# Cross-attention on one core: the probabilities' transposition put ahead of the maxima, x in two buffers

## The chip, the cores and the metric

The kernel runs on one core of a Trainium2 chip. A core has a matrix engine (TensorE, "PE" in the profile; its weight loads are "PEld"), VectorE ("DVE"), ScalarE ("ACT"), GpSimd ("POOL") and SyncE ("SP"). Each of these works through its own list of instructions in order and waits on semaphores for the others. Data lies in SBUF (128 partitions), matrix products come out in PSUM, and DMA queues move data between SBUF and the chip's DRAM; in this kernel nearly all DMAs are issued by SP, whose list holds little else. The metric is the device time of one execution in microseconds (us).

## The reference

The reference is one cross-attention layer. x has 32 batches of 512 rows and 640 channels, the context 32 batches of 77 rows and 1024 channels, and there are 20 heads of 32 channels. With S = 512 and C = 640:

```python
def _sdpa(q, k, v):
    scale = 1.0 / np.sqrt(HD).astype(np.float32)
    s = jnp.einsum('bhqd,bhkd->bhqk', q, k) * scale
    p = jax.nn.softmax(s, axis=-1)
    return jnp.einsum('bhqk,bhkd->bhqd', p, v)
...
q = _heads(hidden_states @ to_q_w)
h_txt = _sdpa(q, _heads(ehs_txt @ to_k_w), _heads(ehs_txt @ to_v_w))
...
out = out @ to_out_w + to_out_b
out = (out + residual) / RESCALE
```

The three other branches (object, others, ip) take the context rows behind the first 77, and there are none, so they add nothing. All is fp32.

## The kernel before, in words

**Precision.** The large products (queries, keys, values of the context, output projection) split each operand into a rounded high part and the low rest, both of type fp32r, and add three products of the parts. ACT makes the high part (a cast), VectorE or POOL the low part (a subtraction).

**Stages.** First the keys and values of all 32 batches are computed and written to DRAM (`k_dram`, `v_dram`). Ahead of that stand matmuls on a tile of zeros (`warm`, L253), which wait for no data. Then comes the main part: a batch has 5 chunks of 128 channels (4 heads), and one chunk of one batch is a *slot*. Slots are numbered n = 0 to 159, with batch b = n div 5 and j = n mod 5; `slot(n)` writes the instructions of one slot, and every engine takes its share of them in the order written. A few instructions after the last slot (`end`) drain the pipeline.

**What a slot does, by the names that the profile uses:**

- `scores(n)` (L410): 32 small matmuls of queries `qt` and keys `kb` into four PSUM tiles `sc`, one for each head. There are only four such tiles, so the scores of a slot need the exponentials of the slot before to be through with them, and they need `copy_q`.
- `maxima(n)` (L422): four VectorE reductions into `nm`, the negated row maxima.
- `exps(n, i)` (L432): for each head 4 ACT exponentials with bias `nm`, each with an instruction that reads out the row sum; 16 of each a slot. Output goes to one of two tiles `pn`, by the parity of n.
- `sums(n)` (L442): a VectorE reciprocal of the row sums. `normalize(n)` (L447): one POOL multiplication over the whole of `pn`.
- `transpose_p(n)` (L454, L461): one VectorE transposition of `pn` in 32x32 blocks into the tile `z`, of which there is one, and four DMAs from `z` to a DRAM tile `pd`. `load_p(n)` (L470) reads `pd` back in one DMA as `raw`, keys on the partitions.
- `values(n)` (L478): 8 matmuls of `raw` and the values `vb` into `pa`; `high_a`, `low_a` (L492, L497) split the result.
- `queries(n + 1)` (L393): 15 matmuls of x and the query weights into `pq`, and `copy_q(n + 1)` (L402), which copies them to `qt` for the next slot: on ACT behind the exponentials in most slots, on VectorE in the first ones.
- `piece(...)` (L515): a part of the output projection of an earlier batch, two pieces a slot; `finish` (L544, L550) adds the residual with bias on VectorE and issues the store of the rows.
- x for the queries: `load_x` (L231) loads a batch in four quarters of 32 partitions, `transpose_x` (L235, VectorE) transposes it in place in four parts (slots j = 0 and 1), and `split_x` (ACT L242, POOL L243) makes the parts that the matmuls read (slots j = 2 and 3). One buffer holds x; a load of the next batch waits until the last split has read the one before.
- `load_residual`, `add_bias` (L504, L508): rows of x again, to which POOL adds the bias a slot later.

**Depth.** In slot n the scores are those of n, the queries those of n + 1, the transposition that of n - 1, `load_p` that of n - 2 and the values those of n - 3 (`taken`). Slots without a projection (`has_out` false: n = 0 to 6) are the *fill*; in slots 0 and 1 the rest of the context's values is computed as well.

**Order.** The scheduler is switched off for all engines (`tc.manual_schedule`), so the order in `slot` is the order on each engine, SP's queue included. In it the transposition of n - 1 stands behind the first half of the exponentials, on VectorE therefore directly behind the maxima of n.

Of the kernel before, what the change touches and what calls it, by code (L numbers as in the profile page):

```python
# [8 lines left out]
F32 = mybir.dt.float32  # L9
# [14 lines left out]
P = 128  # L24
Q = 32
# [12 lines left out]
def kernel(  # L38
# [26 lines left out]
    B, S, C = x.shape  # L65
# [3 lines left out]
    NC_ = C // P  # L69
# [148 lines left out]
    def context_values(g, j, pool):  # L218
        values_of(g, j, pool)
        split_values(g, j)  # L220

    xts, xss, xpool = {}, {}, []

    def load_x(b, quarters=range(4)):

        if b not in xss:
            xss[b] = xpool[0].tile([P, S // Q, C // 4], F32, tag="xs", name="xs")
        xs = xss[b]
        src = x[b].rearrange("(a j) (q u) -> q j a u", j=Q, q=4)
        for q in quarters:  # L230
            nc.sync.dma_start(xs[q * Q : (q + 1) * Q, :, :], src[q])  # L231

    def transpose_x(b, i):
        part = xss[b][:, 4 * i : 4 * i + 4, :].rearrange("p a u -> p (a u)")
        nc.vector.transpose(part, part)  # L235
# [13 lines left out]
    zero = kvt.tile([P, G], FPR, name="zero")  # L249
    nc.vector.memset(zero.bitcast(F32), 0.0)  # L250
    warm = psk.tile([P, G], F32, tag="ps", name="warm")
    for _ in range(12):
        nc.tensor.matmul(warm, zero[:, :P], zero, start=True, stop=True)  # L253

    def first(*ks):
# [126 lines left out]
    def load_keys(b):  # L382
        nc.sync.dma_start(kbs[b % 2], k_dram[:, :, b * NKEY : (b + 1) * NKEY])

    def load_values(b):
        nc.sync.dma_start(vbs[b % 2], v_dram[b * NKEY : b * NKEY + KPAD])

    def queries(n):
        b, j = divmod(n, NC_)
        pqs[n] = ps.tile([P, S], F32, tag="pq", name="pq", bufs=1)  # L390
        for k in range(NC_):
            for m, (a, c) in enumerate(PAIRS):
                nc.tensor.matmul(  # L393
                    pqs[n],
                    wq_s[:, k, a, j * P : (j + 1) * P],
                    xts[b, k][:, c, :],
                    start=(k == 0 and m == 0),
                    stop=(k == NC_ - 1 and m == 2),
                )

    def copy_q(n, copy=nc.scalar.copy):
        copy(qts[n % 2], pqs.pop(n))  # L402

    def scores(n):
        b, j = divmod(n, NC_)
        scs[n] = [ps.tile([P, NQ, P], F32, tag="sc", name="sc", bufs=4) for _ in range(HPC)]
        for t in range(NQ):
            for i, sc in enumerate(scs[n]):
                r = slice(i * HD, (i + 1) * HD)
                nc.tensor.matmul(  # L410
                    sc[:, t, :NKEY],
                    qts[n % 2][r, t * P : (t + 1) * P],
                    kbs[b % 2][r, j, :],
                    start=True,
                    stop=True,
                    tile_position=(i * HD, 0),
                )

    def maxima(n):
        nms[n] = main.tile([P, HPC, NQ], F32, tag="nm", name="nm", bufs=2)  # L420
        for i, sc in enumerate(scs[n]):
            nc.vector.tensor_reduce(  # L422
                nms[n][:, i], sc[:, :, :NKEY], AX.X, ALU.max, negate=True
            )

    def exps(n, i):
        if i == 0:
            sms[n] = main.tile([P, NQ * HPC], F32, tag="sm", name="sm", bufs=2)
        sc = scs[n][i]
        for t in range(NQ):  # L430
            at = t * HPC + i
            nc.scalar.activation(  # L432
                pnb[n % 2][:, at, :NKEY],
                sc[:, t, :NKEY],
                AF.Exp,
                bias=nms[n][:, i, t : t + 1],
                accum_out=sms[n][:, at : at + 1],
            )

    def sums(n):  # L440
        rss[n] = main.tile([P, NQ * HPC], F32, tag="rs", name="rs", bufs=2)
        nc.vector.reciprocal(rss[n], sms.pop(n))  # L442
# [8 lines left out]
    def transpose_p(n):  # L451

        pn = pnb[n % 2]
        nc.vector.transpose(  # L454
            z.rearrange("p b t j -> p t b j"),
            pn.rearrange("p (t h) k -> p t (h k)", t=NQ).rearrange("p t (b i) -> p t b i", i=Q),
        )
        pd = dram.tile([NBLK * Q, S], F32, tag="pd", name="pd", bufs=6)
        rows = pd.rearrange("(b i) q -> i b q", i=Q)
        for a in range(4):  # L460
            nc.sync.dma_start(  # L461
                rows[:, :, a * P : (a + 1) * P],
                z[a * Q : (a + 1) * Q].rearrange("p b t j -> p b (t j)"),
            )
        pds[n] = pd

    def load_p(n):
        pd = pds.pop(n)
        raw = late[0].tile([KPAD, HPC, S], F32, tag="raw", name="raw", bufs=2)
        nc.sync.dma_start(raw, pd.rearrange("(h k) q -> k h q", h=HPC))  # L470
        raws[n] = raw

    def values(n):
        b, j = divmod(n, NC_)
        raw, vb = raws.pop(n), vbs[b % 2][:, j]
        pas[n] = late[1].tile([P, S], F32, tag="pa", name="pa", bufs=1)
        for i in range(HPC):
            nc.tensor.matmul(  # L478
                pas[n][i * HD : (i + 1) * HD, :],
                vb[:, i, :],  # L480
                raw[:, i, :],
                start=True,
                stop=True,
                tile_position=(0, i * HD),
            )
# [15 lines left out]
    def load_residual(b, t, xr=None):  # L501
        if xr is None:
            xr = late[0].tile([P, C], F32, tag="xr", name="xr", bufs=4)
        nc.sync.dma_start(xr, x[b, t * P : (t + 1) * P, :])  # L504
        xrs[b, t] = xr

    def add_bias(b, t):
        nc.gpsimd.tensor_tensor(xrs[b, t], xrs[b, t], bias, ALU.add)  # L508
# [21 lines left out]
    def piece(b, i):  # L530
        for t, h, j in STEPS[CUTS[i] : CUTS[i + 1]]:
            if j == 0:
                output_bank(b, t, h)
            project(b, t, h, j)
            if j == NC_ - 1:
                closed.append((b, t, h))
# [36 lines left out]
    def slot(n, beside=()):  # L573
        b, j = divmod(n, NC_)
        ahead, more = n + 1 < N, b + 1 < B
        back, first = PIECES[j]
        bo_, has_out = b - back, b >= back
        xsplits = SPLIT_X.get(j, ()) if more and n > LATE else ()
        turns = TRANSPOSE_X.get(j, ((), ())) if more and b else ((), ())
        if b == 1 and j < 2:  # L580
            turns = (((), ()), ((0, 1), (2, 3)))[j]
        taken = takes.get(n)
        filling = not has_out

        scores(n)
        if taken is not None:
            values(taken)
        maxima(n)
        if n - LAG + 1 in pds and n > LATE:
            load_p(n - LAG + 1)  # L590
        for k in WO.get(n, ()):
            nc.sync.dma_start(wos[0][:, k].bitcast(F32), wo_dram[:, k].bitcast(F32))
        if j == 0 and more:
            load_keys(b + 1)
        if j == 1:
            load_values(b)
        if n == NC_:
            load_x(b + 1, (2, 3))
        if j == 4 and b and b + 2 < B:
            load_x(b + 2, (0, 1))  # L600
        if j in RESIDUAL and b >= RESIDUAL[j][0]:
            load_residual(b - RESIDUAL[j][0], RESIDUAL[j][1])
        if j in BIAS and b >= BIAS[j][0]:
            add_bias(b - BIAS[j][0], BIAS[j][1])
        if has_out:
            piece(bo_, first)
        for i in range(2):
            exps(n, i)
        if n:
            transpose_p(n - 1)  # L610
        finish()
        if j == 4 and b + 2 < B:
            load_x(b + 2, (0, 1) if not b else (2, 3))
        for i in turns[0]:
            transpose_x(b + 1, i)
        if len(beside) > 1:
            context_values(LAST, beside[1], psv)
        if ahead:
            queries(n + 1)
        if len(beside) > 0:  # L620
            context_values(LAST, beside[0], psv)
        if filling and ahead:
            copy_q(n + 1, nc.vector.tensor_copy)
        for i in range(2, HPC):
            exps(n, i)
        sums(n)
        normalize(n)
        if taken is not None:
            high_a(taken)
        if has_out and ahead:  # L630
            copy_q(n + 1)
        if has_out:
            piece(bo_, first + 1)
        if taken is not None:
            low_a(taken)
        for c in xsplits:
            split_x(b + 1, c)
        for i in turns[1]:
            transpose_x(b + 1, i)
        finish()  # L640
# [128 lines left out]
```

## Time and profile before

| | |
|---|---|
| median of 3 runs | 1797.7 us (1793.98 to 1798.4) |
| profiled execution | 1809.79 us |
| its span, first to last instruction | 1808.0 us |
| TensorE's mean granted clock | 0.987 |
| DMA over the span | 389.12 MB, 215 GB/s |
| busy: PE, ACT, DVE, POOL | 98%, 61%, 52%, 44% |
| first scores (slot 0), scores of slot 7, scores of slot 159 | 264.6, 334.8, 1770.0 us |

A line of the timeline has the start (us from the start of the span), the length, the engine, the line in the kernel, the operation, the names out<-in, the shape, how many instructions were put together, and in brackets the idle time of the engine ahead of it with what ended it. SPq is SP issuing a DMA. A line of the waits has who waited, for whom, the sum in us, how often, and the longest. A line of the windows has the window, its length, each engine's busy time with its number of instructions, the granted clock, the DMA engines' busy share and GB/s. Matmuls are pipelined, so a busy PE need not be PE at its peak.

### The profile page before, as it was taken

The page shows a single profiled execution, that of the slowest core. Times are in us where ns is not written, and L with a number is a line of the kernel's source. Part 1 is how long each engine was busy: PE and PEld are TensorE (multiplying, and loading weights), DVE is VectorE, ACT ScalarE, POOL GpSimd, SP SyncE. Part 2 cuts the span into 40 slices and gives each one's busy share as a digit, 9 for nine tenths or more (in the row PEclk, how much of TensorE's full clock was granted, in tenths as well). Part 3 has the DMA queues.
Part 4 walks back from the last instruction along what each step waited for, and adds up shares of the span by engine and source line. Part 5 has one row for each costly group of instructions (what it writes and reads, how often), then busy time and mean ns, then how long its engine had stood idle before and what let it go on. Part 6 is the DMA issues. An engine that isn't in the chain of part 4 may idle for free.

```text
span 1808.0 us, 39341 instructions
## 1 busy us (share of the span) xinstructions
PE 1763.3 (98%) x13852; PEld 1440.0 (80%) x13852; DVE 933.3 (52%) x1651; ACT 1108.9 (61%) x5698; POOL 789.7 (44%) x502
## 2 busy tenths in 40 slices
PE   8999998899999999999999999999999999999999
PEld 7888896678878888877788777888788888877787
DVE  5233134555555555555555555555555555545553
ACT  3132035666767777767677776677676777666662
POOL 0000034444445555545555545545555555535453
PEclk9999999999999999999999999999999999999999
DMA  9746465899999999998999999998899999898987
GB/s 186 149 94 174 105 168 138 211 231 235 232 232 239 232 243 235 240 235 219 237 232 237 228 230 237 230 233 230 229 234 230 229 240 237 229 224 219 236 207 202
DMA packets 465173, 389.12 MB, mean 215 GB/s; under 512 B 91280, under 2 KB 372368, under 8 KB 464976
## 3 DMA queue, kind: packets, MB, share of 16 engines
q1 hardware_dynamic: 462384, 379.49, 84.5%
q0 software_dynamic: 2496, 6.97, 1.3%
q8 instruction: 109, 1.79, 0.4%
q14 instruction: 88, 0.72, 0.1%
q10 hardware_dynamic: 96, 0.16, 0.0%
HBM read 223.82 MB, written 162.70 MB: 214 GB/s over the span
## 4 chain that ended last, share of the span: by engine, by line
PE 63%; DMA 17%; ACT 6%; POOL 6%; SPq 4%; DVE 2%; issue 2%; POOLq 0%; DVEq 0%; ACTq 0%
PE po L515 20%; PE pq L393 17%; PE pk L177 7%; PE pv L177 7%; DMA raw<-pd 6%; DMA pd<-z 6%; ACT pn L432 6%; PE sc L410 5%; PE pa L478 5%; POOL xt L243 4%; DMA xs<-in_x_dram 4%; SPq L461 2%; POOL pn L447 1%; SPq L231 1%; DVE xs L235 1%
## 5 line engine op out<-in xcount | busy, mean ns | idle before, releaser
L432 ACT ACTIVATE pn<-sc,nm 128x77 f32<-128x77 f32 x2560 | 787.4, 361 | 400.2 <-DVE nm L422 379.6
L515 PEld LDWEIGHTS po<-wo_s,at 128*128 128x128 f32 x3840 | 582.7, 190 | 143.8 <-issue 132.1
L447 POOL TENSOR_TENSOR pn<-pn,rs 128x1232 f32<-128x1232 f32 x160 | 364.0, 2275 | 665.1 <-DVE rs L442 659.9
L515 PE MATMUL po<-wo_s,at 128*128 128x320 f32 x3840 | 636.8, 316 | 0.0
L432 ACT ACTIVATION_READ_ACCUMULATOR pn<-sc,nm 128x1 f32 x2560 | 618.7, 242 | 0.0
L393 PE MATMUL pq<-xt,wq_s 128*128 128x512 f32 x2400 | 582.8, 395 | 0.0
L393 PEld LDWEIGHTS pq<-xt,wq_s 128*128 128x128 f32 x2400 | 450.1, 190 | 92.8 <-issue 4.9
L422 DVE TENSOR_REDUCE nm<-sc 128x4 f32<-128x308 f32 x640 | 261.0, 469 | 202.2 <-PE sc L410 202.1
L454 DVE STREAM_TRANSPOSE z<-pn 128x1280 f32<-128x1280 f32 x160 | 241.1, 1507 | 97.8 <-DMA pd<-z 92.3
L508 POOL TENSOR_TENSOR xr<-xr,bias 128x640 f32<-128x640 f32 x128 | 200.8, 1569 | 94.2 <-DMA xr<-in_x_dram 85.9
L243 POOL TENSOR_TENSOR xt<-xs,xt 128x512 fp32r<-128x512 f32 x160 | 200.0, 1274 | 35.6 <-ACT xt L242 35.6
L478 PE MATMUL pa<-raw,vb 80*32 80x512 f32 x1280 | 173.4, 613 | 27.6 <-DMA raw<-pd 19.6
L410 PEld LDWEIGHTS sc<-kb,qt 32*128 32x128 f32 x5120 | 157.5, 186 | 41.0 <-issue 35.1
L410 PE MATMUL sc<-kb,qt 32*128 32x77 f32 x5120 | 181.0, 277 | 8.7 <-DVE rs L442 5.8
L544 DVE TENSOR_TENSOR xr<-po,xr 128x320 f32<-128x320 f32 x256 | 117.5, 469 | 79.4 <-PE po L515 75.7
L235 DVE STREAM_TRANSPOSE xs<-xs 128x640 f32<-128x640 f32 x128 | 105.8, 832 | 74.2 <-DMA xs<-in_x_dram 74.2
L442 DVE RECIPROCAL rs<-sm 128x16 f32<-128x16 f32 x160 | 38.8, 243 | 196.3 <-ACT pn L432 196.3
L177 PE MATMUL pk<-ct,wk_s 128*128 128x512 f32 (+1 forms) x600 | 136.0, 387 | 3.1 <-ACT wk_s L89 3.1
L402 ACT COPY qt<-pq 128x512 f32<-128x512 f32 x153 | 93.3, 610 | 72.5 <-PE pq L393 72.1
L177 PE MATMUL pv<-ct,wv_s 128*128 128x512 f32 (+1 forms) x600 | 133.9, 381 | 0.0
L177 PEld LDWEIGHTS pk<-ct,wk_s 128*128 128x128 f32 x600 | 114.2, 191 | 23.2 <-ACT wk_s L89 3.6
L497 DVE TENSOR_TENSOR at<-pa,at 128x512 fp32r<-128x512 f32 x160 | 108.6, 679 | 37.2 <-ACT at L492 37.1
(31 smaller groups left out, 536.7 us busy)
## 6 DMA issues: line engine op xcount, KB each, us to landing
pd<-z SPq DMA_DIRECT2D x640, 160.0 KB, 5.4
raw<-pd SPq DMA_DIRECT2D x160, 640.0 KB, 5.5
xs<-in_x_dram SPq DMA_DIRECT2D x128, 320.0 KB, 6.0
xr<-in_x_dram SPq DMA_DIRECT2D x128, 320.0 KB, 5.7
out_dram<-xr SPq DMA_DIRECT2D x127, 320.0 KB, 3.9
vb<-v_dram SPq DMA_DIRECT2D x32, 200.0 KB, 6.0
kb<-k_dram SPq DMA_DIRECT2D x32, 192.5 KB, 7.3
cs<-in_ctx_dram SPq DMA_DIRECT2D x12, 512.0 KB, 9.4
```

The source lines that it names most:

```text
L177: nc.tensor.matmul(held[j][:, :gn], w[:, k, a, :], cts[g, k][:, c, :gn], start=(k == 0 and n == 0), stop=(k == NK - 1 and n == 2),)
L235: nc.vector.transpose(part, part)
L243: low.tensor_tensor(parts[1], src, parts[0].bitcast(F32), ALU.subtract)
L393: nc.tensor.matmul(pqs[n], wq_s[:, k, a, j * P : (j + 1) * P], xts[b, k][:, c, :], start=(k == 0 and m == 0), stop=(k == NC_ - 1 and m == 2),)
L410: nc.tensor.matmul(sc[:, t, :NKEY], qts[n % 2][r, t * P : (t + 1) * P], kbs[b % 2][r, j, :], start=True, stop=True, tile_position=(i * HD, 0),
L422: nc.vector.tensor_reduce(nms[n][:, i], sc[:, :, :NKEY], AX.X, ALU.max, negate=True)
L432: nc.scalar.activation(pnb[n % 2][:, at, :NKEY], sc[:, t, :NKEY], AF.Exp, bias=nms[n][:, i, t : t + 1], accum_out=sms[n][:, at : at + 1],)
L447: nc.gpsimd.tensor_tensor(pf, pf, rs.unsqueeze(2).to_broadcast([P, NQ * HPC, NKEY]), ALU.mult)
L454: nc.vector.transpose(z.rearrange("p b t j -> p t b j"), pn.rearrange("p (t h) k -> p t (h k)", t=NQ).rearrange("p t (b i) -> p t b i", i=Q),)
L478: nc.tensor.matmul(pas[n][i * HD : (i + 1) * HD, :], vb[:, i, :], raw[:, i, :], start=True, stop=True, tile_position=(0, i * HD),)
L508: nc.gpsimd.tensor_tensor(xrs[b, t], xrs[b, t], bias, ALU.add)
L515: nc.tensor.matmul(pos[b, t, h][:, :HALF], ats[b * NC_ + j][:, a, t * P : (t + 1) * P], wos[0][:, j, c, h * HALF : (h + 1) * HALF], start= ...
```

## The change

It has four parts.

- From slot 7 on, `transpose_p(n - 1)` is written ahead of `maxima(n)`, behind `load_p`; its four DMAs thereby come ahead of the loads of keys, values, x and residual on SP's queue. In slots 1 to 6 it stays where it was.
- x has two buffers. The loads for batch b + 2 are issued as one quarter in each of the slots j = 1 to 4 of batch b (for batch 2: two quarters in slot 4 and two in slot 5), where they were two pairs in slot j = 4 from the second batch on.
- In slots 3 to 6 the values stand behind the queries instead of behind the scores.
- The warming matmuls are 22 instead of 12.

```diff
@@ load_x
-            xss[b] = xpool[0].tile([P, S // Q, C // 4], F32, tag="xs", name="xs")
+            xss[b] = xpool[0].tile([P, S // Q, C // 4], F32, tag="xs", name="xs", bufs=2)
...
-    for _ in range(12):
+    for _ in range(22):
         nc.tensor.matmul(warm, zero[:, :P], zero, start=True, stop=True)
@@ slot
         scores(n)
-        if taken is not None:
+        if taken is not None and has_out:
             values(taken)
-        maxima(n)
         if n - LAG + 1 in pds and n > LATE:
             load_p(n - LAG + 1)
+        if n and has_out:
+            transpose_p(n - 1)
+        maxima(n)
...
-        if n == NC_:
-            load_x(b + 1, (2, 3))
-        if j == 4 and b and b + 2 < B:
-            load_x(b + 2, (0, 1))
+        if b + 2 < B:
+            quarters = {4: (0, 1), 5: (2, 3)}.get(n, ()) if n <= NC_ else (j - 1,) if j else ()
+            if quarters:
+                load_x(2 if n <= NC_ else b + 2, quarters)
...
         for i in range(2):
             exps(n, i)
-        if n:
+        if n and not has_out:
             transpose_p(n - 1)
         finish()
-        if j == 4 and b + 2 < B:
-            load_x(b + 2, (0, 1) if not b else (2, 3))
...
         if ahead:
             queries(n + 1)
+        if taken is not None and not has_out:
+            values(taken)
```

## The prediction

> **What bounds the kernel now.** I read the page first, then the windows, then the timeline of single slots, and last the waits. A slot is one batch's 128 channels: 5 slots a batch, n = 0 to 159, j = n mod 5.
>
> ```profile
> span 1808.0 us, 39341 instructions
> PE 1763.3 (98%) x13852; PEld 1440.0 (80%) x13852; DVE 933.3 (52%) x1651; ACT 1108.9 (61%) x5698; POOL 789.7 (44%) x502
> ```
>
> TensorE (PE) is taken nearly all the time and no other engine is over 61%. What that hides is whether anything else turns at nearly the same pace. One steady slot, n = 47, with the start of the next:
>
> ```profile
> 710.55 1.13 PE L410 MATMUL sc<-kb,qt 32*128 32x77 f32 x32
> 711.70 1.63 DVE L422 TENSOR_REDUCE nm<-sc 128x4 f32<-128x308 f32 x4 [0.55 <-PE sc L410]
> 712.27 0.33 ACT L432 ACTIVATE pn<-sc,nm 128x77 f32<-128x77 f32 x1 [2.72 <-DVE nm L422]
> 713.52 1.51 DVE L454 STREAM_TRANSPOSE z<-pn 128x1280 f32<-128x1280 f32 x1 [0.18 <-DMA pd<-z]
> ...
> 716.99 0.29 ACT L432 ACTIVATION_READ_ACCUMULATOR pn<-sc,nm 128x1 f32 x1
> 717.32 0.25 DVE L442 RECIPROCAL rs<-sm 128x16 f32<-128x16 f32 x1 [2.29 <-ACT pn L432]
> 717.72 2.28 POOL L447 TENSOR_TENSOR pn<-pn,rs 128x1232 f32<-128x1232 f32 x1 [4.50 <-DVE rs L442]
> 719.75 1.13 PE L410 MATMUL sc<-kb,qt 32*128 32x77 f32 x32
> 720.90 1.63 DVE L422 TENSOR_REDUCE nm<-sc 128x4 f32<-128x308 f32 x4 [2.41 <-PE sc L410]
> ```
>
> The reader is to see two things. The scores come every 719.75 - 710.55 = 9.20 us (9.19 in most slots): that is TensorE's own work. And the normalization of slot 47 (POOL) ends at 717.72 + 2.28 = 720.00, 0.25 after slot 48 has begun; its transposition today waits behind the maxima, where that costs nothing. Over all slots from 7 on, the first whose transposition is moved:
>
> ```profile
> 334.78:1770.00 1435.22, 171.91 (x4865) 149.41 (x4865) 0.99 0.91 231
> 336.74 1.59 DVE L422 TENSOR_REDUCE nm<-sc 128x4 f32<-128x308 f32 x4
> 1771.15 1.63 DVE L422 TENSOR_REDUCE nm<-sc 128x4 f32<-128x308 f32 x4 [0.93 <-PE sc L410]
> ```
>
> The first row, of the windows for the scores alone, counts 4865 score matmuls, 152 slots of 32 and one. The maxima of slot 7 begin at 336.74 and those of slot 159 at 1771.15: 1434.4 us, of which 152 x 9.19 = 1396.9 is TensorE's pace and 37.5 is stalls. These sit almost all in slots with j = 1; slot 91, in the timeline:
>
> ```profile
> 1124.26 1.13 PE L410 MATMUL sc<-kb,qt 32*128 32x77 f32 x32
> 1127.19 1.39 PE L478 MATMUL pa<-raw,vb 80*32 80x512 f32 x8 [1.80 <-DMA raw<-pd]
> 1136.83 0.44 PE L410 MATMUL sc<-kb,qt 32*128 32x77 f32 x5
> ```
>
> and two windows (length; busy time of each engine; granted clock, DMA share, GB/s), the one after that stall and the one around slot 86:
>
> ```profile
> 1077.20:1087.20 10.00, 9.09 (x79) 7.42 (x79) 7.62 (x15) 6.08 (x34) 4.28 (x2) 1.00 0.87 208
> 1127.81:1131.22 3.41, 3.41 (x17) 2.71 (x11) 1.51 (x1) 3.41 (x25) 0.00 (x0) 0.50 0.48 116
> ```
>
> Slot 91 takes 1136.83 - 1124.26 = 12.57 us: 1.80 waiting for the probabilities' return from DRAM, and some 1.6 because the granted clock is 0.50 for the next 3.41 us. In slot 86 TensorE idled 0.91 and the clock stayed at 1.00.
>
> **Step 1, the transposition ahead of the maxima.** VectorE works in the order written (above: maxima, transposition, reciprocal, as in the code). With the move, maxima(n) stand behind transposition(n-1), which waits for normalization(n-1), which waits for the 16 exponentials of n-1, which wait for maxima(n-1). That closes a ring over four steps on three engines, one turn a slot. Two links are not in slot 47 (after POOL, before the next VectorE instruction); the fill of the pipeline shows the first (a transposition that POOL released), slot 44 the second:
>
> ```profile
> 292.53 2.29 POOL L447 TENSOR_TENSOR pn<-pn,rs 128x1232 f32<-128x1232 f32 x1
> 294.85 1.51 DVE L454 STREAM_TRANSPOSE z<-pn 128x1280 f32<-128x1280 f32 x1 [1.70 <-POOL pn L447]
> ...
> 685.23 1.50 DVE L454 STREAM_TRANSPOSE z<-pn 128x1280 f32<-128x1280 f32 x1
> 686.66 0.48 DVE L544 TENSOR_TENSOR xr<-po,xr 128x320 f32<-128x320 f32 x1
> ```
>
> Maxima to first exponential 712.27 - 711.70 = 0.57; exponentials to 716.99 + 0.29 = 717.28, 5.01; reciprocal 0.04 later, 0.25 long; normalization 0.15 later, 2.28 long; transposition 0.03 after it (294.85 - 294.82); next VectorE instruction 1.43 after its start (686.66 - 685.23). Sum 9.76 us. TensorE needs 9.19, so the ring sets the pace: +0.57 in each of 152 slots, **+86.2**. TensorE itself then idles 0.57 a slot, ahead of the scores.
>
> What else is late? Scores need the copy of the queries, on ACT behind the exponentials:
>
> ```profile
> 726.20 0.29 ACT L432 ACTIVATION_READ_ACCUMULATOR pn<-sc,nm 128x1 f32 x1
> 726.75 0.69 ACT L402 COPY qt<-pq 128x512 f32<-128x512 f32 x1
> ```
>
> Copied 0.95 after the last exponential (726.49 to 727.44), the scores can begin at 1.10 (0.15 for the release, as POOL's by the reciprocal), are done at 2.23, and the maxima, by the ring, start at 4.18 (0.04 + 0.25 + 0.15 + 2.28 + 0.03 + 1.43): cover of 1.9. The values of slot n-3 and both projection pieces stay inside TensorE's 9.19. Of VectorE's other work, the values' low half, a closing addition and, at j = 0 and 1, an x transposition lie between reciprocal and transposition; I take them to fit into the 2.46 that the normalization fills there (0.15 + 2.28 + 0.03).
>
> **Step 2, DMAs.** Each slot from 7 on moves its four pd writes ahead of the key, value, x and residual loads on SP's queue, and x comes as one 320 KB quarter a slot at j = 1 to 4 instead of two pairs in j = 4. SP now stands at the pd writes until the transposition is done; behind them wait the loads, and behind those the next slot's read of raw. Keys, values and x are needed a batch later; the residual's bias is added by POOL a slot later, and its normalization is due only 6.0 us after that slot's maxima begin. The pairs are what made j = 1 late: in slot 44 they are issued just ahead of and behind the pd writes.
>
> ```profile
> 686.51 0.85 SPq L231 DMA_DIRECT2D xs<-in_x_dram  x2
> 687.94 3.05 SPq L461 DMA_DIRECT2D pd<-z  x4
> 691.67 1.69 SPq L231 DMA_DIRECT2D xs<-in_x_dram  x2
> 695.55 1.51 DVE L454 STREAM_TRANSPOSE z<-pn 128x1280 f32<-128x1280 f32 x1 [1.04 <-DMA pd<-z]
> 704.81 1.51 DVE L454 STREAM_TRANSPOSE z<-pn 128x1280 f32<-128x1280 f32 x1 [1.11 <-DMA pd<-z]
> ```
>
> The buffer z is single: a transposition waits until the last pd write of the one before has landed. From a transposition's end that took 704.81 - 697.06 = 7.75 us with a pair of x behind the writes before, and 695.55 - 686.73 = 8.82 with a pair just ahead of the writes. The ring allows 9.76 - 1.51 = 8.25. Now there is one quarter, behind the writes, which is nearest to the first: I take no wait. Bounds: 0, and 8.82 - 8.25 = 0.57 in every slot. A slot's traffic, 231 GB/s x 9.44 us = 2.18 MB, takes 223 GB/s at 9.76, under the 231 of the window. The raw read gets as much time as before. So the **37.5** us of stalls go; the cover is the ring, which is later than the DMAs. VectorE's waits for x (below) go too, since the last quarter is issued a slot before its transposition; off the path they are worth nothing.
>
> **Step 3, the fill (slots 0 to 6).** There the transposition stays where it was, and the values go behind the queries. The pace of slots 3 to 6 is z's:
>
> ```profile
> 313.04 2.71 SPq L461 DMA_DIRECT2D pd<-z  x4
> 315.80 1.86 SPq L231 DMA_DIRECT2D xs<-in_x_dram  x2
> 340.31 1.51 DVE L454 STREAM_TRANSPOSE z<-pn 128x1280 f32<-128x1280 f32 x1 [1.98 <-DMA pd<-z]
> ```
>
> Values behind queries free TensorE, but the next scores wait for a VectorE copy behind these transpositions, so I book nothing. x's first pair in slot 4 now goes ahead of the pd writes (1.86 of issues, some 1 us of landing), and slot 6 gets a quarter more ahead of its writes (320 KB at 231 GB/s = 1.4): the last z of the fill comes not at 340.31 but near 342.3. And slot 7 is the first whose maxima stand behind it: 342.3 + 1.43 = 343.7 instead of 336.74, **+7.0** (bounds +4 and +10).
>
> **Step 4, warming.**
>
> ```profile
> 1.46 4.58 PE L253 MATMUL warm<-zero 128*128 128x512 f32 x12 [1.46 <-DVE zero L250]
> 9.16 6.43 PE L177 MATMUL pk<-ct,wk_s 128*128 128x512 f32 x15 [3.12 <-ACT wk_s L89]
> 8.00:16.00 8.00, 6.84 (x18) 5.26 (x19) 5.88 (x10) 3.48 (x8) 0.00 (x0) 0.57 1.04 202
> 17.49 3.56 PE L177 MATMUL pk<-ct,wk_s 128*128 128x512 f32 x15
> ```
>
> Twelve matmuls end at 6.04, and the first 15 key matmuls take 6.43 at a granted clock of 0.57, against 3.56 later. Ten more at 3.56 / 15 = 0.24 end near 8.4, before 9.16, and the clock should hold: the gain is at most 2.9, less some waiting for the weights' low half. I take **-2.0** (bounds -2.9, and +1.2 if the ten ran at the first twelve's 0.38 to 0.43 and held up the keys). The Trainium skill ("TensorE: Matmul & The Clock Gate", part 1) has the clock fall after an idle window of about 3.4 us; by it the gap of 3.12 us would not cool the array, ten more matmuls would be worth 0, and the sum would be 2.0 higher. The trace does not agree: the clock had fallen after that gap, and in slot 91 after a stall of 1.80.
>
> **Step 5, the end.** After the scores of slot 159 (at 1770.00) TensorE has its work without a gap, to the last group, 60 matmuls with no idle ahead:
>
> ```profile
> 1795.15 9.07 PE L515 MATMUL po<-wo_s,at 128*128 128x320 f32 x60
> ```
>
> These scores now lead their maxima by 4.18 - 1.10 = 3.08 instead of 1.15: **-1.9**. Two x buffers in themselves cost nothing.
>
> **The sum**: +86.2 - 37.5 + 7.0 - 2.0 - 1.9 = +51.8, on the profiled execution's 1809.8 (its span of 1808.0 and 1.8 around it): 1861.6. That execution lies 12.1 above the median of the runs, 1797.7. If the 12.1 are DMA waits, they go with the 37.5 and the run comes out at 1861.6; if they are spread evenly, at 1849.2. I take the middle, 1855.
>
> **The rivals.** *Waits for z join the ring.* For it: 7.7 against 8.25 is thin. Against: less x and later. Each 0.1 us a slot is 15 us; at 0.2 the time is 1885. *The idle cools the array.* TensorE now stops 0.57 us in every slot. Against: slot 86, whose 0.91 left the clock at 1.00. The price is slot 91's 12.57 - 9.19 - 1.80 = 1.58 a slowed slot: TensorE would need 10.77, over the ring's 9.76 by 1.0; a slowed slot has no idle, so it is every second one, 0.5 a slot, 77 us: 1932. The Trainium skill (same page, "A second HAM failure mode: psum-queue depth-cycling") describes such micro-idles between groups of matmuls as making the clock swing. *Faster: the ring does not bind.* The profile may lengthen the 32 small ACT instructions of a slot. If their 5.01 us are 4.44 or less without it, the ring is at 9.19, TensorE sets the pace, and the stalls still go: 1797.7 - 37.5 + 7 - 2 = 1765. For it: the 12.1 us by which the profiled run is longer; against: TensorE sets the pace in both, and 0.57 is 11% of those instructions.
>
> **How the numbers follow.** The forecast has 0.77, waits for z 0.12, cooling 0.03, the ring not binding 0.08 (0.06 faster, 0.02 about even, on the way there). Within 0.3% is about what a measurement of this kernel cannot tell from no change. So faster 0.06, same 0.02, slower 0.92. The range goes down to 1835 (even spread, a ring shorter by 0.1, 15 us) and up to 1888 (z waits of 0.2 a slot); it leaves out the faster case, cooling, and a part of the rest.
>
> **What would show it.** Scores 9.76 apart from slot 7 on; transposition 0.03 after POOL's normalization, maxima 1.43 after that, in every slot; TensorE's largest wait becomes scores for ACT's copy, near 0.57 x 152 = 87 us; VectorE's wait of z for pd falls from 92.3 (78 times) to some tens at most, that for x from 74.2 to near 0; no slot at j = 1 longer than its neighbours; keys at full clock from 9.16. Scores 9.19 apart would refute step 1, z waiting for pd step 2.
>
> ```profile
> DVE z L454 <- DMA pd<-z: 92.3, 78, 5.5
> DVE xs L235 <- DMA xs<-in_x_dram: 74.2, 30, 5.3
> ```

## The result, and the profile after

The changed kernel takes 1860.1 us (median; 1859.2 to 1865.3) against 1798.05 for the kernel before on the same chip: 1.0356 times as long, 95% interval [1.0331, 1.0380]. (Ratios are those on record; they differ by up to 0.3% from the quotient of the two medians.) The profiled execution has a span of 1863.2 us and took 1865.3; before, 1808.0 and 1809.8.

The page of the changed kernel, its span, its engines and the chain that ended last, and below them that chain in the kernel before:

```profile
span 1863.2 us, 39459 instructions
PE 1770.6 (95%) x13862; PEld 1437.0 (77%) x13862; DVE 924.8 (50%) x1651; ACT 1097.0 (59%) x5698; POOL 791.0 (42%) x502
...
ACT 39%; POOL 18%; PE 17%; DVE 12%; issue 9%; DMA 3%; SPq 2%; POOLq 0%; ACTq 0%; DVEq 0%
```

```profile
PE 63%; DMA 17%; ACT 6%; POOL 6%; SPq 4%; DVE 2%; issue 2%; POOLq 0%; DVEq 0%; ACTq 0%
```

TensorE held 63% of that chain before and holds 17% now. ACT, POOL and VectorE hold 69%, though none of them is busy more than 59%: they do not work more, they wait for each other in turn. That is what a ring looks like on a page. The timeline of one steady slot (n = 48) and the start of the next shows it link by link:

```profile
741.25 1.13 PE L410 MATMUL sc<-kb,qt 32*128 32x77 f32 x32 [0.44 <-ACT qt L402]
742.96 1.51 DVE L454 STREAM_TRANSPOSE z<-pn 128x1280 f32<-128x1280 f32 x1 [1.53 <-POOL pn L447]
744.40 1.59 DVE L422 TENSOR_REDUCE nm<-sc 128x4 f32<-128x308 f32 x4
744.93 0.33 ACT L432 ACTIVATE pn<-sc,nm 128x77 f32<-128x77 f32 x1 [2.70 <-DVE nm L422]
...
749.65 0.29 ACT L432 ACTIVATION_READ_ACCUMULATOR pn<-sc,nm 128x1 f32 x1
749.97 0.25 DVE L442 RECIPROCAL rs<-sm 128x16 f32<-128x16 f32 x1 [3.18 <-ACT pn L432]
750.37 2.27 POOL L447 TENSOR_TENSOR pn<-pn,rs 128x1232 f32<-128x1232 f32 x1 [3.42 <-DVE rs L442]
750.96 1.13 PE L410 MATMUL sc<-kb,qt 32*128 32x77 f32 x32 [0.48 <-ACT qt L402]
752.67 1.51 DVE L454 STREAM_TRANSPOSE z<-pn 128x1280 f32<-128x1280 f32 x1 [1.14 <-POOL pn L447]
```

The scores and the first transposition aside (POOL ended slot 47's normalization at 742.93), each link starts when the one above it lets it, by a semaphore or by the order on its engine: maxima to first exponential 0.53, exponentials 5.01 (to 749.94), 0.03, reciprocal 0.25, 0.15, normalization 2.27, 0.03, transposition to maxima 1.44. The sum is 9.71, and the scores come 750.96 - 741.25 = 9.71 apart. They are done 2 us before the maxima may start (742.38 against 744.40).

All slots from 12 to 159, in the windows of the scores (window, length, PE and PEld busy, granted clock, DMA share, GB/s), and the waits that answer to those of before:

```profile
391.63:1820.19 1428.56, 166.25 (x4705) 144.50 (x4705) 1.00 0.90 224
```

```profile
DVE z L454 <- POOL pn L447: 158.3, 154, 1.7
PE sc L410 <- ACT qt L402: 69.7, 148, 3.3
DVE z L454 <- DMA pd<-z: 20.3, 5, 6.2
DVE xs L235 <- DMA xs<-in_x_dram: 4.2, 1, 4.2
```

4705 matmuls are 147 slots and one: 9.718 us a slot where it was 9.42 with the stalls and 9.19 without. The transposition waits for POOL 154 times, for DMAs 5 times (78 before), x for its load once (30 before). Where the 55.2 us between the two spans come from, cut at the maxima of slots 7 and 159:

| stretch | before | after | difference |
|---|---|---|---|
| start to the scores of slot 0 | 264.62 | 262.13 | -2.5 |
| scores of slot 0 to the maxima of slot 7 | 72.12 | 82.08 | +10.0 |
| maxima of slot 7 to those of slot 159: 152 turns at 9.19, then 9.711 | 1396.9 | 1476.1 | +79.2 |
| stalls in that stretch (what is longer than the turns) | 37.5 | 3.0 | -34.5 |
| maxima of slot 159 to the end | 36.86 | 39.89 | +3.0 |

### The profile page after: what moved, and what is told of

It is laid out like the page before. It is cut to its first block, busy times and chain, and to the rows that moved or that the text cites. A ratio compares the mean times of both kernels' runs of the same rounds, so it can differ in the third digit from the quotient of the medians.

```text
span 1863.2 us, 39459 instructions
## 1 busy us (share of the span) xinstructions
PE 1770.6 (95%) x13862; PEld 1437.0 (77%) x13862; DVE 924.8 (50%) x1651; ACT 1097.0 (59%) x5698; POOL 791.0 (42%) x502
## 4 chain that ended last, share of the span: by engine, by line
ACT 39%; POOL 18%; PE 17%; DVE 12%; issue 9%; DMA 3%; SPq 2%; POOLq 0%; ACTq 0%; DVEq 0%
ACT pn L432 39%; POOL pn L447 18%; PE pv L177 7%; PE pk L177 7%; DVE z L454 6%; DVE nm L422 3%; DVE rs L442 2%; DMA pd<-z 2%; PE po L515 1%; SPq L461 1%; PE pq L393 1%; DMA out_dram<-xr 1%; PE pa L478 0%; DMA xr<-in_x_dram 0%; DMA wraw<-in_L_xattn_to_k_w_dram 0%
## 5 line engine op out<-in xcount | busy, mean ns | idle before, releaser
L410 PE MATMUL sc<-kb,qt 32*128 32x77 f32 x5120 | 183.1, 279 | 82.3 <-ACT qt L402 69.7
L422 DVE TENSOR_REDUCE nm<-sc 128x4 f32<-128x308 f32 x640 | 255.4, 456 | 5.2 <-PE sc L410 5.2
L177 PEld LDWEIGHTS pv<-ct,wv_s 128*128 128x128 f32 x600 | 113.9, 190 | 19.3
L492 ACT CAST at<-pa 128x512 fp32r<-128x512 f32 x160 | 107.6, 672 | 22.5 <-PE pa L478 22.5
```

The source lines that it names most:

```text
L177: nc.tensor.matmul(held[j][:, :gn], w[:, k, a, :], cts[g, k][:, c, :gn], start=(k == 0 and n == 0), stop=(k == NK - 1 and n == 2),)
L410: nc.tensor.matmul(sc[:, t, :NKEY], qts[n % 2][r, t * P : (t + 1) * P], kbs[b % 2][r, j, :], start=True, stop=True, tile_position=(i * HD, 0),
L422: nc.vector.tensor_reduce(nms[n][:, i], sc[:, :, :NKEY], AX.X, ALU.max, negate=True)
```

## The experiments

In every run the kernel before ran on the same chip; its medians there were 1805.3 (first four runs), 1810.9 (the next four) and 1807.6 us (the last three), so times of different groups are compared by their ratios.

### The transposition put back, all else as changed

```diff
-        if n and has_out:
-            transpose_p(n - 1)
         maxima(n)
...
-        if n and not has_out:
+        if n:
             transpose_p(n - 1)
```

> All of the change but its first part: the transposition of slots 7 to 159 stands where it stood before, behind the maxima. Theory (a ring over VectorE, ACT and POOL sets the pace, because the maxima stand behind the transposition): the ring opens, scores come every 9.19 us again, and with x in quarters most of the 37.5 us of stalls at j = 1 stay away: a span of 1770 to 1790 us. Rival (SP's queue or the x loads by quarters cost the time): x still comes by quarters, so the span stays above 1840.

Measured: 1855.4 us, ratio 1.0264 [1.0226, 1.0302], span 1856.8. The span missed the expected range by 67 us, and the rival stated with it named the number. Yet the ring did open: 94 of the 147 turns from slot 12 on are within 0.1 us of 9.19 again. The loss now sits in stalls, 86 us in place of 37.5 between the maxima of slots 7 and 159. The windows of the scores for slots 12 to 159, SP and VectorE in the timeline around slots 76 and 77, then the waits:

```profile
386.56:1818.74 1432.18, 166.31 (x4704) 144.54 (x4705) 0.99 0.90 224
```

```profile
1013.98 0.30 SPq L470 DMA_DIRECT2D raw<-pd  x1
1014.34 0.87 SPq L386 DMA_DIRECT2D vb<-v_dram  x1
1015.30 0.38 SPq L231 DMA_DIRECT2D xs<-in_x_dram  x1
1015.73 0.48 SPq L504 DMA_DIRECT2D xr<-in_x_dram  x1
1016.26 2.63 SPq L461 DMA_DIRECT2D pd<-z  x4
...
1024.71 1.51 DVE L454 STREAM_TRANSPOSE z<-pn 128x1280 f32<-128x1280 f32 x1 [2.19 <-DMA pd<-z]
```

```profile
DVE z L454 <- DMA pd<-z: 338.0, 140, 6.5
```

As soon as the last write has landed (1013.98), SP issues the read of raw, then this slot's values, the quarter of x and the residual, and only then the next four writes, which land at 1024.7. From landing to landing that is 10.7 us, over TensorE's 9.19, in a kernel with one z. So there is a second ring, through z and SP, and with the x quarter ahead of the writes it is longer than TensorE's turn. Undoing the first part of the change had also moved the writes back behind the loads: one edit, two effects.

### The quarter moved behind the writes

Against the run above:

```diff
-        if b + 2 < B:
-            quarters = ...
-            if quarters:
-                load_x(2 if n <= NC_ else b + 2, quarters)
...
         if n:
             transpose_p(n - 1)
+        if b + 2 < B:
+            quarters = ...
+            if quarters:
+                load_x(2 if n <= NC_ else b + 2, quarters)
```

> The kernel with the transposition back behind the maxima, whose stalls grew to 85 us, with the x quarter moved behind the transposition and its pd writes on SP. Theory: with the quarter ahead of the writes, the last one landed 7.9 us (median) after the transposition's end, and 1.51 + 7.9 = 9.45 is over TensorE's 9.19, a second ring over z and SP; with the quarter behind, the landing falls to about 6, and the scores come every 9.19 with few stalls: 1770 to 1790 us. Rival (a quarter in every slot costs time wherever it stands): above 1830.

Measured: 1770.4 us, ratio 0.9798 [0.9775, 0.9821], span 1770.7. The windows of the scores for slots 12 to 159, the waits, and the issue of pd (median us from issue to landing at the end of the row):

```profile
381.41:1732.72 1351.31, 166.25 (x4705) 144.48 (x4705) 1.00 0.93 237
```

```profile
DVE z L454 <- DMA pd<-z: 13.9, 5, 3.9
```

```profile
pd<-z SPq DMA_DIRECT2D x640, 160.0 KB, 4.1
```

1351.31 / 147 = 9.193: every one of these slots is at TensorE's pace, at 237 GB/s. In the kernel with the quarter ahead, a pd write took 6.5 us to land. The same bytes, with one load at another place on SP's queue, make 86 us of stalls or 3. Residual, keys and values still stand ahead of the writes here; only the quarter has moved.

### One reduction ahead of the transposition

```diff
-        if n and has_out:
-            transpose_p(n - 1)
-        maxima(n)
+        maxima(n, (0,))
+        if n and has_out:
+            transpose_p(n - 1)
+        maxima(n, range(1, HPC))
```

> The changed kernel with one of the four reductions (head 0) ahead of the transposition and three behind it. The pd writes are still early on SP. Theory: four of the 16 exponentials (1.25 us of ACT) no longer wait for the transposition, the ring falls from 9.71 to about 8.5, under TensorE's 9.19, and scores come every 9.19 us: 1765 to 1790 us. Rival (SP standing at the early pd writes, with the loads behind it, costs the time): 9.71 stays, 1850 to 1865 us.

Measured: 1776.5 us, ratio 0.9837 [0.9811, 0.9863], span 1774.7. VectorE at the opening of a slot, and the windows of the scores for slots 12 to 159:

```profile
707.78 0.48 DVE L424 TENSOR_REDUCE nm<-sc 128x4 f32<-128x308 f32 x1 [0.55 <-PE sc L410]
708.17 1.50 DVE L456 STREAM_TRANSPOSE z<-pn 128x1280 f32<-128x1280 f32 x1
```

```profile
384.89:1736.20 1351.31, 1.00 0.95 237
```

9.193 again. The pd writes are as early on SP as in the changed kernel, the transposition too; only 0.4 us of VectorE work has changed places with it, and from slot 12 on the whole loss is gone. That isolates the ring: what counts is which instruction stands behind which, and no engine does less.

### The ring made longer, and the same work outside it

In the changed kernel, and in the one above (there in the second call of `maxima`), head 3 is reduced twice. The edit of the changed kernel:

```diff
-        maxima(n)
+        maxima(n, (3, 0, 1, 2, 3) if has_out else range(HPC))
```

> The changed kernel with one more reduction a slot (head 3 is reduced twice, first and last, with the same result), directly behind the transposition; VectorE is busy half the time, so it has room for it. Theory: a link of 0.39 more (1.59 / 4) in the ring is paid in every slot: scores 10.1 apart, +59 us, 1920 us. Rival (the pace is set by DMAs, SP or TensorE's clock): 0 to 10 us more than the changed kernel.

> The kernel with one reduction ahead of the transposition, with the same one reduction more a slot behind it that cost 0.41 in every slot of the changed kernel. Theory: the ring is about 8.5 there, 0.7 under TensorE's 9.19, so 0.41 more stays under it: scores 9.19 apart, the same time as without it, 1776 us, plus 0 to 5. Rival (each VectorE instruction at the slot's opening costs its length, ring or not): 1776 + 62 = 1838.

Measured: in the ring 1923.7 us, ratio 1.0649 [1.0618, 1.0681], span 1918.3, 55.1 over the changed kernel's. VectorE, in the timeline of the longer ring:

```profile
704.93 1.51 DVE L456 STREAM_TRANSPOSE z<-pn 128x1280 f32<-128x1280 f32 x1 [1.53 <-POOL pn L449]
706.37 1.98 DVE L424 TENSOR_REDUCE nm<-sc 128x4 f32<-128x308 f32 x5
715.06 1.51 DVE L456 STREAM_TRANSPOSE z<-pn 128x1280 f32<-128x1280 f32 x1 [1.14 <-POOL pn L449]
```

One turn is 10.13, and 0.39 more of reductions (1.98 against 1.59) costs 0.41 a slot: 59.9 us in slots 12 to 159 (1488.48 against 1428.56). Ahead of slot 12 and behind the scores of slot 159 this execution is 2.2 and 2.7 us shorter than the changed kernel's, which makes the 55.1. With one reduction ahead, the same work gives 1781.6 us, ratio 0.9863 [0.9842, 0.9884]; its slots stay at 9.19:

```profile
392.14:1743.60 1351.46, 1.00 0.94 237
```

Its span is 7.9 over that without it, but from slot 12 on (1351.46 against 1351.31) nothing is lost: 7.3 of it lie before slot 12. Of these, 3.1 are there at the scores of slot 7, before the added reduction has run once, and 1.6 of the 3.1 are slot 1's slow clock (last section). Another 3.2 are slot 8, at a granted clock of 0.57 from 352 to 359 us, where the run without the reduction has 1.00. Whether the added reduction has a part in slot 8 was not tried. So, in the steady slots, 0.4 us of the same engine is paid in full inside the ring, and not at all once the ring is shorter than TensorE's turn.

### The move alone

```diff
 kernel before, with
-        maxima(n)
         if n - LAG + 1 in pds and n > LATE:
             load_p(n - LAG + 1)
+        if n and has_out:
+            transpose_p(n - 1)
+        maxima(n)
...
-        if n:
+        if n and not has_out:
             transpose_p(n - 1)
```

> The kernel before with the first part alone: the transposition ahead of the maxima from slot 7 on; x in one buffer and two pairs, 12 warming matmuls, values where they were. Theory: scores 9.71 apart or more from the ring; a pair of x near the pd writes makes z wait inside the ring now, about 0.6 us once a batch (18 us), and the wait for x on VectorE ahead of the reciprocal counts too: 1860 to 1890 us. Rival (x by quarters is what costs): 1790 to 1810 us.

Measured: 1888.5 us, ratio 1.0460 [1.0427, 1.0492], span 1884.7. As expected, stalls come on top of the ring, 28 us of them between the maxima of slots 7 and 159, mostly in slots with j = 1 and 2; VectorE in the timeline at such a place (slot 41):

```profile
673.25 0.84 DVE L235 STREAM_TRANSPOSE xs<-xs 128x640 f32<-128x640 f32 x1 [2.45 <-DMA xs<-in_x_dram]
...
678.26 1.51 DVE L454 STREAM_TRANSPOSE z<-pn 128x1280 f32<-128x1280 f32 x1 [1.59 <-DMA pd<-z]
```

Both pairs of x stand behind the writes of their slot, but ahead of the next ones (issued at 668.90); these land later than the ring, and z waits 1.59. Before the change such a wait cost nothing as long as the transposition was still in time, now every one of them shifts the maxima. The changed kernel has 3 us of stalls there, so the other parts of the change, the x loads by what the waits name, give some 25 us back that the move would cost on top.

### Warming alone, and the fill alone

```diff
-    for _ in range(12):
+    for _ in range(22):
```

> The kernel before with 22 warming matmuls instead of 12 and nothing else. Theory: no half clock at 8 to 15 us, the first scores 2.0 to 2.5 us earlier (264.6 to about 262.3), and the rest unchanged but for the phase of clock windows: -2 us, -0.1%. Rival (a gap of 3.1 us does not cool the array): 0, first scores at 264.6.

Measured: 1801.5 us, ratio 0.9965 [0.9946, 0.9985], with the first scores at 262.20 instead of 264.62. The runs show a gain, of 0.15% to 0.54%, some 3 to 10 us; the stretch up to the first scores explains 2.4 of it, and the rest stays open. The other profiles say how far 2.4 can be trusted: with 12 warming matmuls the first scores came at 264.62 (before), 263.78, 263.25 and 263.24 (`e2_move_only`, `g2_x_only_behind`, `f8_fill_only`), the clock between 8 and 16 us being 0.57 in the first and 0.79 in the other three. With 22 they came at 262.12 to 262.40 in all nine profiles, at 1.00. So the gain is 0.8 to 2.5 us, and the profile from which it was forecast is the slowest of the four. That profile also has more stalls between the maxima of slots 7 and 159: 37.5 us, against 33.0 in this run and 30.1 in the next, whose slots there are the same.

```diff
-        if taken is not None:
+        if taken is not None and has_out:
             values(taken)
...
             queries(n + 1)
+        if taken is not None and not has_out:
+            values(taken)
```

> The kernel before with the values of slots 3 to 6 behind the queries and nothing else. Theory as predicted: worth nothing, -1 to +1 us, since the scores of these slots wait for a VectorE copy behind a transposition that waits for DMAs. Rival: the queries no longer wait for raw, slots 3 and 4 get shorter by 1 to 2 us each and it stays so: -3 us.

Measured: 1805.7 us, ratio 0.9990 [0.9970, 1.0010]: no difference that these runs resolve, but the rival's -3 us (0.17%) lies inside the interval. The trace speaks against it: from the first scores to those of slot 10 it took 100.06 us (263.24 to 363.30), and 98.93 in the kernel before (264.62 to 363.55).

### x alone, with the quarter behind the writes, and with the warming

The kernel before with two x buffers and the quarter behind the transposition, and the same with 22 warming matmuls (that is, the kernel with the quarter behind, less the fill part):

> The kernel before with x in two buffers and one quarter a slot, issued behind the pd writes; transposition, fill and 12 warming matmuls as before. Theory: the stalls at j = 1 (30 to 37 us in the profiles of before) go, with no ring: scores 9.19 apart in all slots from 8 on, 2 to 3 us more than with 22 warming matmuls: 1770 to 1775 us. Rival (the gain of the x loads hangs on the other parts): above 1785.

> The kernel with the transposition behind the maxima and the x quarter behind its writes, with the values of slots 3 to 6 put back behind the scores. Theory: the fill part of the change is worth nothing or costs up to 2 us: 1767 to 1771 us. Rival (it brings 3 us): 1773.

Measured: x alone 1770.7 us, ratio 0.9808 [0.9768, 0.9847]; with the warming 1768.5, ratio 0.9796 [0.9761, 0.9831]. Both run at 9.193 a slot. The gain that the change holds lies in x's two buffers and quarters, provided that they stand behind the writes; what warming adds is inside the intervals here. The second has the lowest time, 2.0% under the kernel before and, by the ratios (0.9796 / 1.0356), 5.4% under the changed one; the intervals do not tell it from x alone or from the kernel with the quarter behind the writes (0.9798).

### The move in slots 10 to 154 alone

```diff
-        if n and has_out:
+        if 10 <= n < 155:
             transpose_p(n - 1)
...
-        if n and not has_out:
+        if n and not 10 <= n < 155:
             transpose_p(n - 1)
```

> The changed kernel with the transposition ahead of the maxima in slots 10 to 154 alone. Theory: 145 turns of the ring in place of 152 (-4 us); the maxima no longer stand behind the fill's last transpositions (-6 to -9 us); and TensorE no longer leads VectorE at the end, so its stall of 1.86 us for an output bank and the slow clock behind it go (the stretch from the maxima of slot 159 to the end falls from 39.9 to about 37): 1843 to 1850 us by the profile. Rival (fill and end cost the same wherever the move begins and ends): 1856 to 1860 us.

Measured: 1856.9 us, ratio 1.0281 [1.0246, 1.0316], span 1853.5, between the theory's 1843 to 1850 and the rival's 1856 to 1860. For the end the theory holds: from the maxima of slot 159 it takes 36.9 us, as before the change. For the fill the rival holds: the first moved slot, now 10, has its maxima at 371.82, 7.1 after its scores (364.72) instead of 1.15, because its transposition waits there for the pd writes of the one before (6.84 us); in slot 7 it was the same wait (below). The switch to the early transposition costs its 6 to 8 us once, at both places where it was made.

## Why the prediction was right, and where not

**Step 1, the ring: right, its size 0.05 too large.** 9.71 instead of 9.76: the first exponential starts 0.53 after the maxima's start, not 0.57. That is 79.2 us instead of 86.2. TensorE's idle time ahead of the scores is 0.47 a slot (69.7 / 148), close to the 0.52 by which the ring is longer than 9.19. Three runs bear the ring out by themselves: opened by 0.4 us of reordering it is gone, lengthened by 0.4 it costs 0.41 a slot, and with the ring below TensorE's turn the same 0.4 costs nothing a slot.

**Step 2, DMAs: the number right (-34.5 for -37.5), the reason only half.** "The cover is the ring, which is later than the DMAs" falls: at TensorE's own pace, without the ring, the stalls are gone as well (one reduction ahead; quarter behind). With x by quarters, the order on SP decides: 86 us of stalls with the quarter ahead of the writes, 3 with it behind. The order alone is not enough either: the move alone has its x behind the writes too, in pairs, and kept 28 us. Whether pairs behind the writes would do at TensorE's own pace was not run. The prediction did count on the quarter standing behind the writes ("nearest to the first"); the expectation of the first experiment did not, and missed by it. The 34.5 are also measured against a profile with more stalls than two others of the same main loop (33.0 and 30.1).

**Step 3, the fill: too small, at its upper bound.** +10.0 instead of +7.0. The values behind the queries brought nothing, as booked. The last z of the fill and the maxima behind it, in the timeline of the changed kernel:

```profile
342.77 1.51 DVE L454 STREAM_TRANSPOSE z<-pn 128x1280 f32<-128x1280 f32 x1 [6.25 <-DMA pd<-z]
344.21 1.59 DVE L422 TENSOR_REDUCE nm<-sc 128x4 f32<-128x308 f32 x4
```

Predicted were 342.3 and 343.7, and with the 2 us of warming that should have been 340.3 and 341.7. That the maxima of slot 7 stand 1.44 behind this z was right. Counted from the first scores, the z came 4.95 us later than before, not 2.0: 1.6 of the 2.95 are slot 1's slow clock (last section); the rest was not taken apart, and the loads of x ahead of the writes are the likeliest. The prediction named 1.86, 1 and 1.4 us for these, and took 2.0 for their sum of 4.3 without saying why.

**Step 4, warming: right, with an open size.** -2.5 for -2.0 in this pair of profiles, 0.8 to 2.5 over all of them. The timeline and the windows:

```profile
1.45 6.79 PE L253 MATMUL warm<-zero 128*128 128x512 f32 x22 [1.45 <-DVE zero L250]
9.01 4.11 PE L177 MATMUL pk<-ct,wk_s 128*128 128x512 f32 x15 [0.77 <-ACT wk_s L89]
```

```profile
8.00:16.00 8.00, 7.10 (x31) 5.37 (x30) 6.26 (x11) 4.03 (x9) 0.00 (x0) 1.00 1.07 209
```

The warming now ends at 8.24, 0.77 ahead of the keys, and the clock between 8 and 16 is 1.00 where it was 0.57. By the rule of the Trainium skill that the prediction weighed ("TensorE: Matmul & The Clock Gate", part 1) it would have been 1.00 with 12 as well; the trace decides for the row.

**Step 5, the end: the wrong sign.** +3.0 instead of -1.9. The step took for granted that a TensorE which leads VectorE ends earlier. TensorE, VectorE and a window of the changed kernel's end:

```profile
1822.24 6.43 PE L515 MATMUL po<-wo_s,at 128*128 128x320 f32 x42
1830.53 1.78 PE L515 MATMUL po<-wo_s,at 128*128 128x320 f32 x6 [1.86 <-DVE xr L544]
1828.92 0.25 DVE L442 RECIPROCAL rs<-sm 128x16 f32<-128x16 f32 x1 [3.58 <-ACT pn L432]
1830.00 0.48 DVE L544 TENSOR_TENSOR xr<-po,xr 128x320 f32<-128x320 f32 x1
```

```profile
1830.80:1837.60 6.80, 6.80 (x27) 4.81 (x27) 3.07 (x4) 0.58 (x1) 2.28 (x2) 0.50 0.70 173
```

The projection's next bank comes free by VectorE's closing addition at 1830.00, which stands in order behind the reciprocal, which waits for the ring's exponentials. TensorE, ahead by 3.15, stops 1.86 us for it, and then runs 6.8 us at half clock. Its last group of 60 matmuls starts 30.19 us after the scores of slot 159 (1820.19 to 1850.38), 25.15 before (1770.00 to 1795.15); the longer lead gives 2.0 of these 5.0 us back. The lead became a wait. With the last five slots left unmoved the stall does not occur and the end is 36.9.

**The sum and the median.** +55.2 on the span against +51.8. That this is so near is partly luck: the terms miss by -7.0 (ring), +3.0 (DMAs), +3.0 (fill), -0.5 (warming) and +4.9 (end), and cancel to +3.4 (the ring's 86.2 is itself 152 x 0.567, where 0.57 would give 86.6). Of the two ways to carry it to the median, the first was nearer (1861.6; measured 1860.1): the profiled execution now lies 5.2 above the median, before 11.7. If all of these 5.2 us sat in the ring, it would be 0.03 a turn shorter in the other executions; the middle of 1855 was 5 too low.

**The rivals.** Waits for z did not join the ring: 5 in all, 20.3 us, none of them behind slot 12. The idle did not cool the array: the clock is 1.00 over the 1428.56 us, with 0.47 idle in nearly every slot. What the Trainium skill says of micro-idles ("TensorE: Matmul & The Clock Gate", "A second HAM failure mode: psum-queue depth-cycling") was not seen at this size. The ring did bind.

## What to carry to other kernels

Before an instruction is moved ahead of another on an in-order engine, follow what it waits for back to the last turn of the loop: if the chain comes back to the instruction that it is put in front of, add up the links, and compare the sum with the turn of the busiest engine, not with the idle shares. Do the same for each buffer that a DMA has to empty, with everything that its queue issues in between. An undo that moves DMAs along with the instruction tests two things at once.

## What the runs showed of the hardware that was not expected

The same stall lowers TensorE's granted clock in one execution and not in another. In slot 1 TensorE idles 1.38 us ahead of the scores in both kernels. In the changed one the clock is halved behind it and the next 24 matmuls take 6.35 us:

```profile
272.77 1.13 PE L410 MATMUL sc<-kb,qt 32*128 32x77 f32 x32 [1.38 <-DVE rs L442]
273.84 6.35 PE L177 MATMUL pv<-ct,wv_s 128*128 128x416 f32 x24
```

```profile
274.30:277.70 3.40, 3.40 (x11) 3.26 (x11) 1.71 (x5) 3.23 (x22) 2.87 (x2) 0.50 0.99 386
```

The kernel before, at the same place, has the same idle and 4.75:

```profile
275.26 1.13 PE L410 MATMUL sc<-kb,qt 32*128 32x77 f32 x32 [1.38 <-DVE rs L442]
276.32 4.75 PE L177 MATMUL pv<-ct,wv_s 128*128 128x416 f32 x24
```

So slot 1 gave back 1.6 of the 2.5 us that the warming had gained in this pair of profiles. It is not the earlier start that does it. All nine profiles with 22 warming matmuls reach these scores at 272.77 to 273.05 us, and from them to the scores of slot 2 five take 16.7 us (the changed kernel among them) and four 15.1 (with `f7_warm_only`, where the 24 matmuls take 4.76). What goes along with it is the idle time ahead of the first key matmuls: 0.63 to 0.86 us in the five, 0.39 or less in the four. Whether that is a cause was not tried.
